# Layer 0 of a four-layer graph network: another opening, with the diagonal read from converted adjacency, the bias moved, wide loads of x and the table written by GpSimd

## Chip, cores and metric

The kernel runs on one core of one Trainium2 chip. The metric is the device time of one execution in microseconds (us). A core has five engines with queues of their own: TensorE (PE; its weight loads are listed as PEld), VectorE (DVE), ScalarE (ACT), GpSimd (POOL) and SyncE (SP). SP and ACT also issue transfers, which run on 16 DMA engines; GpSimd issues its own, and only it issues the indirect ones (gathers and scatters by a list of rows).

## What is computed

There are 3327 nodes with 256 values each (`x`) and a symmetric adjacency matrix of int32 with ones on its diagonal, about 1% full. Four attention layers follow each other, each as `x = layernorm(x + layer(x, adj))`. The change touches layer 0 alone:

```python
def _L0_gnn_ref(nodes, adj_mat, W_src_w, W_src_b, W_tgt_w, W_tgt_b, a_w):
    g_src = nodes @ W_src_w.T + W_src_b
    g_tgt = nodes @ W_tgt_w.T + W_tgt_b
    g = g_src[:, None, :] + g_tgt[None, :, :]
    g = jax.nn.leaky_relu(g, NEG_SLOPE)
    score = jnp.einsum('ijc,c->ij', g, a_w)
    score = jnp.where(adj_mat != 0, score, -jnp.inf)
    weights = jax.nn.softmax(score, axis=1)
    return weights @ g_tgt
...
x = _layernorm(x + _L0_gnn_ref(x, adj, ...), axis=-1)
```

The leaky relu stands inside the dot product with `a_w`, so a score can't be split into a part of i and a part of j. Layers 1 to 3 have scores that can, and are computed densely on the transposed adjacency.

## The kernel before

Layer 0 (`sparse0`, from L269) works on lists of neighbours. The rows are cut into 26 tiles of 128 (the last has 127), in four groups ("sets") of 4, 7, 9 and 6 tiles.

**The table.** `targets(it)` (L400) loads 128 columns of the transposed x on SP (`xt`, L386), projects them on TensorE (L391, product `pt`), adds the bias `bt_rows` on VectorE into `row` (L409), and ScalarE's queue writes the row to a table in DRAM (`table_d`, L410). For the first four tiles it is also written to `own0_d` (L412). `sources(it)` (L417) does the same with the other weight, adding its bias by a matmul with a row of ones (L396), and writes the negated product to the group's `own{s}_d` (L429). A row of `own{s}_d` holds the negated source, x and the target of one node. The x part is copied from DRAM to DRAM (L126 is the line of the helper `copy_rows`): on GpSimd's queue for the first group, on SP's for the others. The target part of the later groups is copied from the table by SP.

**The lists.** `neighbours(s)` (L462) is a generator. For each tile of its group it loads the adjacency rows in pieces of 1024 columns (SP, L126, `adj_i`, three buffers), ScalarE turns them into bf16 (L492, `adj_b`) and counts them, TensorE makes column numbers of the ones in banks of 512 columns (L502, L505; the node's own column is taken out by L510, product `v`, three PSUM buffers), and VectorE takes maxima of 8 over chunks of about 104 (`scan`, L522). `sort` (L525) draws the 56 largest from these, `note` (L537) makes the payload: the list, the node's number, and its diagonal flag from `own_marks`. The flag comes from `diag_i`, 3327 single elements of the adjacency loaded on ScalarE's queue (L351), which `mark_own` (L361) spreads. Then `key`, `spread_key` and `keep_key` make sort keys, and the nodes of a group are ranked by the number of their neighbours (L621), so that a tile needs only as many places as its fullest row. The first group's lists are put in order by matmuls (`permute`, L631), the others' by indirect writes and a read on GpSimd (`write_list`, `read_lists`).

**The gathers.** For each tile and each place k, GpSimd gathers 128 rows of the table (L730, 945 in all), four places to a part `g`, 22 buffers of a part. The own rows come by one gather for a tile (L718). VectorE forms `max(target, minus)` (L750) and its weighted sum (L756), ScalarE the exponentials and the scaled rows (L803), TensorE adds the rows up (L806). `add_input` (L826) adds the normalized sum to x; `put_back` (L840) scatters it to `sums{s}_d`. Gathers run 8 parts ahead of the scores. Small GpSimd work is put between two gathers through the list `between`, one item after every second gather (L736).

**What sets the order.** In layer 0 the order on TensorE, VectorE, ScalarE and GpSimd is the program's; SP's is left to a scheduler. The opening is the loop at L961: for each of the 26 tiles, `targets` is run to its end, and `next(first)` twice steps the first group's generator. Then the main loop at L1038 steps the generators of the later groups between the scores, as far as due times ask for it.

Of the kernel before, what the change touches and what calls it, by code (L numbers as in the profile page):

```python
# [8 lines left out]
F32 = mybir.dt.float32  # L9
# [40 lines left out]
def gat_stack(  # L50
# [218 lines left out]
    def sparse0(lost):  # L269
        GROUP, TURNS, LEAD, SPREAD = 4, 22, 8, 8  # L270
        starts = [sum(SETS[:s]) for s in range(len(SETS))]
        with ExitStack() as s0:
# [12 lines left out]

            w_tgt = const0.tile([P, kc, ROW], F32, name="w_tgt0")
            nc.sync.dma_start(w_tgt[:, :, :dim], w_tgt_t.rearrange("(c p) f -> p c f", p=P))
            nc.vector.memset(w_tgt[:, :, dim:], 0.0)
            a_row = load_row(const0, a_w, "a_row")
            bt_rows = const0.tile([P, ROW], F32, name="bt_rows")  # L290
            nc.vector.memset(bt_rows[:, dim:], 0.0)
            nc.sync.dma_start(
                bt_rows[:, :dim],
                bass.AP(tensor=b_tgt.tensor, offset=b_tgt.offset, ap=[[0, P], [1, dim]]),
            )
            w_src = const0.tile([P, kc, dim + 1], F32, name="w_src0")
            nc.scalar.dma_start(w_src[:, :, :dim], w_src_t.rearrange("(c p) f -> p c f", p=P))
            nc.vector.memset(w_src[:, :, dim:], 0.0)
            bs_row = const0.tile([1, dim + 1], F32, name="bs_row")
            nc.vector.memset(bs_row[:, dim:], BIG)  # L300
            nc.sync.dma_start(bs_row[:, :dim], b_src[None])
            for c in range(kc):
                t = io0.tile([P, dim], F32, tag="minus", name="dots0")
                nc.vector.tensor_mul(t, w_tgt[:, c, :dim], a_row)
                nc.vector.tensor_reduce(w_tgt[:, c, dim : dim + 1], t, axis=AX.X, op=ALU.add)
            nc.vector.tensor_scalar_mul(
                w_tgt[:, :, dim], w_tgt[:, :, dim], SLOPE
            )
            ones = const0.tile([P, P], F32, name="ones")
            nc.vector.memset(ones, 1.0)  # L310
            a_ps = ps0.tile([P, BANK], F32, tag="a", name="a_ps", bufs=1)
            nc.scalar.mul(a_ps[:, :dim], a_row, 1.0 - SLOPE)
            nc.scalar.copy(a_ps[:, dim : dim + 1], ones[:, :1])
# [5 lines left out]
            PIECE = 2 * BANK  # L319
            pieces = [(lo, min(n, lo + PIECE)) for lo in range(0, n, PIECE)]  # L320
            code = const0.tile([65, BANK], BF16, name="code")
            nc.vector.memset(code, 0.0)
            nc.vector.memset(code[64:65, :], 1.0)
            for row, pattern in ((0, [[16, BANK // 16], [0, 16]]), (32, [[0, BANK // 16], [1, 16]])):
                digit = io0.tile([P, PIECE], I32, tag="adj_i", name="digit", bufs=3)
                nc.gpsimd.iota(digit[:33, :BANK], pattern=pattern, base=0, channel_multiplier=0)
                nc.vector.tensor_copy(code[row : row + 1, :], digit[row : row + 1, :BANK])
# [5 lines left out]
            digit = io0.tile([P, PIECE], I32, tag="adj_i", name="digit", bufs=3)  # L333
# [13 lines left out]
            diag_i = const0.tile([P, nt], I32, name="diag_i")  # L347
            nc.vector.memset(diag_i, 0)
            for lo, hi in ((0, n // P), (n // P, nt)):
                if lo < hi:  # L350
                    nc.scalar.dma_start(  # L351
                        diag_i[: min(P, n - lo * P), lo:hi],
                        bass.AP(
                            tensor=adj.tensor, offset=adj.offset + lo * P * (n + 1),
                            ap=[[n + 1, min(P, n - lo * P)], [P * (n + 1), hi - lo]],
                        ),
                    )
# [3 lines left out]
            def mark_own():  # L361
# [100 lines left out]
            def neighbours(s):  # L462
# [121 lines left out]
                for k in all_pieces[:3]:  # L584
                    load(*k)
# [1264 lines left out]
```

## Time and profile before

| | us |
|---|---|
| median of three runs (3083.48 to 3091.56) | 3086.51 |
| the profiled execution | 3087.03 |
| its span, first to last instruction | 3085.2 |
| first conversion of adjacency on ScalarE (L492) starts | 30.76 |
| first gather of own rows (L718) starts | 128.25 |
| first gather of the table (L730) starts | 143.38 |
| last gather of the table starts | 1435.9 |
| last write-back of layer 0 (L843) starts | 1461.59 |

Lines of the timeline and of the chain of waits give a start and a length in us, then the engine (with a q behind it where its queue issues a transfer), the line of the kernel, the operation, output <- input, and how often; in brackets is the idle time before it and what ended it. A group of instructions has the mean length of one in ns behind its sum in us, then the idle time before such instructions with what ended it. A line of GpSimd's waits gives the sum in us, the number and the longest one. A line of windows gives, for each engine, busy us and number of instructions.

### The profile page before, as it was taken

How to read it: one execution, taken by the hardware profiler on the slowest of the kernel's cores; microseconds unless marked ns; L12 is line 12 of the kernel's file. 1: busy time of each engine (PE TensorE's matmuls, PEld its weight loads, DVE VectorE, ACT ScalarE, POOL GpSimd, SP SyncE). 2: the span in 40 equal slices, each digit the busy share in tenths (PEclk: the TensorE clock that was granted, in tenths of full speed). 3: DMA queues.
4: the chain of work that ended last, by engine and by line, in shares of the span. 5: the costliest groups of instructions: out<-in, count | busy, mean ns of one | idle time of the engine just before them, and what ended most of it. 6: DMA issues, size and time to landing. Idle time of an engine off the chain costs nothing.

```text
span 3085.2 us, 45364 instructions
## 1 busy us (share of the span) xinstructions
PE 2335.1 (76%) x16026; PEld 1293.6 (42%) x16046; DVE 2139.3 (69%) x5551; ACT 861.5 (28%) x2400; POOL 1014.8 (33%) x1073
## 2 busy tenths in 40 slices
PE   4547656544456423645899999989999999999996
PEld 2313222211222111322788888874434545434332
DVE  4499997777777536654355531129888889899997
ACT  1126544442344322534334421110110110120110
POOL 0177777777777777775000000000000000000000
PEclk8658768776677766868999999999999999999998
DMA  7676676455744436543776643341212212212211
GB/s 190 171 194 191 187 173 170 128 141 142 157 130 113 113 106 118 138 111 90 240 243 200 199 119 91 104 126 46 69 44 71 70 46 71 67 46 61 57 47 46
DMA packets 192883, 372.17 MB, mean 121 GB/s; under 512 B 38719, under 2 KB 135055, under 8 KB 191624
## 3 DMA queue, kind: packets, MB, share of 16 engines
q1 hardware_dynamic: 110668, 179.09, 20.8%
q0 software_dynamic: 51520, 156.84, 20.2%
q10 hardware_dynamic: 30460, 33.25, 3.2%
q8 instruction: 130, 2.13, 0.3%
q14 instruction: 105, 0.86, 0.1%
HBM read 329.27 MB, written 46.12 MB: 122 GB/s over the span
## 4 chain that ended last, share of the span: by engine, by line
PE 46%; DVE 4%; DMA 1%; issue 0%; ACT 0%; SPq 0%; POOL 0%; DVEq 0%; POOLq 0%; ACTq 0%
PE acc L1505 18%; PE acc L1458 16%; PE acc L1513 9%; PE misc L1304 3%; DVE e L1374 2%; DMA at<-at_d 1%; PE misc L1401 0%; PE misc L1587 0%; PE misc L1548 0%; DMA dst<-in_l_a_dram 0%; DVE stats L1665 0%; DVE h L1663 0%; DVE both L1660 0%; DVE h L248 0%; DVE h L1478 0%
## 5 line engine op out<-in xcount | busy, mean ns | idle before, releaser
L730 POOL DMA_INDIRECT g<-table_d,lst x945 | 898.0, 950 | 309.7 <-issue 256.3
L1374 DVE SCALAR_TENSOR_TENSOR e<-rate,feat,at 128x896 f32<-128x896 f32 (+4 forms) x832 | 844.1, 1079 | 80.8 <-PE acc L1513 69.7
L806 PE MATMUL acc<-g,ident 128*128 128x512 f32 x958 | 519.0, 688 | 353.8 <-ACT g L803 310.1
L1505 PE MATMUL acc<-e,feat 128*32 128x384 f32 (+2 forms) x6656 | 688.6, 516 | 4.8 <-DVE e L1374 2.1
L806 PEld LDWEIGHTS acc<-g,ident 128*128 128x128 f32 x958 | 203.2, 221 | 590.3 <-ACT g L803 462.4
L750 DVE TENSOR_TENSOR y<-g,minus_ps 128x1028 f32<-128x1028 f32 (+2 forms) x245 | 288.9, 1179 | 223.4 <-DMA g<-table_d,lst 211.9
L1505 PEld LDWEIGHTS acc<-e,feat 128*32 128x32 f32 x6656 | 259.3, 110 | 342.2 <-issue 231.4
L803 ACT ACTIVATE g<-g,w 128x256 f32<-128x256 f32 x945 | 389.5, 495 | 10.3 <-DMA h<-sums_d 4.9
L1513 PE MATMUL acc<-e,feat 128*32 128x384 f32 (+3 forms) x3328 | 375.4, 512 | 0.0
L756 DVE SCALAR_TENSOR_TENSOR y<-y,a_ps 128x257 f32<-128x257 f32 x945 | 342.7, 418 | 7.5
L1458 PE MATMUL acc<-feat,e 128*128 128x257 f32 (+2 forms) x1352 | 306.5, 384 | 16.2 <-DMA at_i<-in_adj_t_dram 13.3
L1458 PEld LDWEIGHTS acc<-feat,e 128*128 128x128 f32 (+2 forms) x1352 | 257.3, 192 | 54.4 <-issue 14.3
L242 POOL TENSOR_TENSOR rstds<-rstds,minus_half 128x7 f32<-128x7 f32 (+1 forms) x12 | 19.7, 1644 | 777.5 <-DVE rstds L241 777.5
L502 PE MATMUL v<-code,leads 65*128 65x512 bf16 (+1 forms) x182 | 84.5, 465 | 222.7 <-DVE cand L522 185.2
L1458 PE MATMUL acc<-feat,at 128*128 128x257 bf16 (+2 forms) x2028 | 239.6, 275 | 7.9 <-DMA at<-at_d 7.7
L1458 PEld LDWEIGHTS <-at 128*128 128x128 bf16 (+2 forms) x2028 | 199.6, 100 | 42.7 <-DMA at<-at_d 5.6
L1513 PEld LDWEIGHTS acc<-e,feat 128*32 128x32 f32 (+1 forms) x3328 | 139.6, 110 | 156.8 <-issue 132.7
L1374 DVE SCALAR_TENSOR_TENSOR e<-rate,feat,at_i 128x896 f32<-128x896 f32 (+2 forms) x104 | 111.6, 1080 | 75.2 <-DMA at_i<-in_adj_t_dram 43.0
L522 DVE MAX8 cand<-v 128x8 f32<-128x104 f32 (+2 forms) x858 | 158.6, 260 | 6.2 <-PE v L505 6.0
L1354 POOL DMA_DIRECT2D rate3b_d<-rate_rows x4 | 2.1, 524 | 468.3 <-ACT rate_rows L1353 468.3
L502 PEld LDWEIGHTS <-leads 65*128 65x128 bf16 x182 | 20.3, 112 | 260.3 <-DVE cand L522 210.9
L492 ACT ACTIVATE adj_b<-adj_i 128x1024 bf16<-128x1024 int32 (+1 forms) x104 | 92.5, 889 | 111.4 <-DMA diag_i<-in_adj_dram 23.5
(199 smaller groups left out, 1740.6 us busy)
## 6 DMA issues: line engine op xcount, KB each, us to landing
adj_i<-in_adj_dram SPq DMA_DIRECT2D x75, 512.0 KB, 4.6
at<-at_d SPq DMA_DIRECT2D x150, 224.0 KB, 2.5
at_i<-in_adj_t_dram SPq DMA_DIRECT2D x50, 448.0 KB, 4.6
g<-table_d,lst POOLq DMA_INDIRECT x945, 2.9
at<-at_d SPq DMA_DIRECT2D x75, 192.0 KB, 2.4
at<-at_d SPq DMA_DIRECT2D x75, 191.8 KB, 2.4
at_d<-at ACTq DMA_DIRECT2D x50, 224.0 KB, 4.2
at_i<-in_adj_t_dram SPq DMA_DIRECT2D x25, 384.0 KB, 3.4
```

The source lines that it names most:

```text
L502: nc.tensor.matmul(v[:, :w], leads[:, b, :], code[:, :w], start=True, stop=False)
L522: nc.vector.max(spread[:, c0 + c, :], view(v[:, :w]))
L730: nc.gpsimd.indirect_dma_start(out=g[:, k - k0, :], out_offset=None, in_=table_d[:, :], in_offset=bass.IndirectOffsetOnAxis(ap=entry["lst" ...
L750: nc.vector.tensor_tensor(y, rows, minus_src[:, None, :].to_broadcast([P, m, dim + 1]), op=ALU.max)
L756: nc.vector.scalar_tensor_tensor(y, y, 1.0, a_ps[:, : dim + 1], op0=ALU.mult, op1=ALU.mult, accum_out=sc)
L803: nc.scalar.activation(rows, rows, AF.Copy, scale=w[:, k : k + 1])
L806: nc.tensor.matmul(dst, ident, rows, start=start, stop=stop)
L1304: nc.tensor.matmul(pacc[:pn, : dim + self.extra], ht[:, k, :pn], self.weight[:, k, :], start=(k == 0), stop=(k == kc - 1),)
L1374: nc.vector.scalar_tensor_tensor(e[:pn, : c1 - c0], self.rate[b][:pn, h_of, : c1 - c0], q, at[:pn, : c1 - c0], op0=ALU.max, op1=ALU.mult,)
L1458: nc.tensor.matmul(accs[s][:pn, : dim + 1], a[:pj, s * P : s * P + pn], f[:pj, : dim + 1], start=(j == 0 and part == 0), stop=(j == nt - 1 ...
L1505: nc.tensor.matmul(accs[x][p][q : q + 32, : hi - lo], f[:pj, at0 : at0 + 32], es[at0 // hd][:pj, lo:hi], start=(j == 0), stop=(j == nt - 1),)
L1513: nc.tensor.matmul(accs[x][pairs][h_of * 32 : (h_of + 1) * 32, : hi - lo], f[:pj, dim + h_of : dim + h_of + 1].to_broadcast([pj, 32]), es[ ...
```

## The change

Six things are changed in layer 0, and nothing else:

- **Diagonal.** `diag_i`, its loads and `mark_own` are gone. In `fill`, VectorE multiplies the 128x128 block of converted adjacency on the diagonal with the identity and sums the rows into `own_marks`.
- **Bias of the targets.** It is no longer added to the table's rows. It is added to the sources' bias, and, since the weights of a row sum to one, to the x part of `own{s}_d`, by an accumulating transfer on GpSimd's queue: the first group's at the start, the others' between gathers.
- **Wide x.** In the opening x is loaded as seven pieces of 512 columns on ScalarE's queue, into buffers of the gathers that are needed last, instead of 128 columns at a time on SP's.
- **Table.** ScalarE copies the product to `row`; GpSimd's queue writes it.
- **Targets one behind.** The copy of tile `it` follows the matmuls of tile `it + 1`, and the generator is stepped once and twice in turn.
- **Adjacency first.** The first three pieces are the first transfers of SP's queue; weights, rows and biases move to ScalarE's. The iotas use another buffer.

```diff
+            for p in range(3):
+                load(0, 0, p)
             w_tgt = const0.tile([P, kc, ROW], F32, name="w_tgt0")
-            nc.sync.dma_start(w_tgt[:, :, :dim], w_tgt_t.rearrange("(c p) f -> p c f", p=P))
+            nc.scalar.dma_start(w_tgt[:, :, :dim], w_tgt_t.rearrange("(c p) f -> p c f", p=P))
...
+            def columns_wide(b):
+                lo, hi = banks_n[b]
+                t = gath.tile(
+                    [P, GROUP, ROW], F32, tag=f"g{(TURNS - 1 - b + SHIFT) % TURNS}", name="x_wide"
+                )
...
+                nc.scalar.dma_start(t[:, :, : hi - lo], x_t_p[:, :, lo:hi])
+            columns_wide(0)
             w_src = const0.tile([P, kc, dim + 1], F32, name="w_src0")
             nc.scalar.dma_start(w_src[:, :, :dim], w_src_t.rearrange("(c p) f -> p c f", p=P))
...
+            nc.scalar.dma_start(bias[:, 0, :dim], b_src[None])
+            nc.scalar.dma_start(bias[:, 1, :dim], b_tgt[None])
+            for b in range(1, len(banks_n)):
+                columns_wide(b)
...
-                    nc.scalar.dma_start(
-                        diag_i[: min(P, n - lo * P), lo:hi],
...
+            def keep_inputs(s, engine):
+                lo, hi = starts[s] * P, min(n, (starts[s] + SETS[s]) * P)
+                copy_rows(engine, own_d[s][: hi - lo, AT_X : AT_X + dim], x[lo:hi, :])
+
+            def add_bias(s):
+                lo, hi = starts[s] * P, min(n, (starts[s] + SETS[s]) * P)
+                nc.gpsimd.dma_start(
+                    own_d[s][: hi - lo, AT_X : AT_X + dim],
+                    b_tgt[None].to_broadcast([hi - lo, dim]), accum_op=ALU.add,
+                )
+
+            keep_inputs(0, nc.gpsimd)
+            add_bias(0)
...
+                nc.vector.tensor_add(bs_row[:, :dim], bs_row[:, :dim], bias[:, 1, :dim])
...
             def columns_of(it):
+                if not placed:
+                    b, at0 = divmod(it * P, BANK)
+                    return wide_x[b][:, :, at0 : at0 + pn], pn
...
-                nc.vector.tensor_add(row[:pn], pt[:pn, :ROW], bt_rows[:pn])
-                nc.scalar.dma_start(table_d[1 + it * P : 1 + it * P + pn, :], row[:pn])
+                nc.scalar.copy(row[:pn], pt[:pn, :ROW])
+                nc.gpsimd.dma_start(table_d[1 + it * P : 1 + it * P + pn, :], row[:pn])
...
+                        flag = io0.tile([P, P], BF16, tag="flag", name="flag", bufs=1)
+                        nc.vector.scalar_tensor_tensor(
+                            flag[:, :wo], adj_b[:, own0 % PIECE : own0 % PIECE + wo], 1.0,
+                            ident[:, :wo], op0=ALU.mult, op1=ALU.mult,
+                            accum_out=marks[:, starts[s] + t, 1:2],
+                        )
...
             first = neighbours(0)
+            next(first)
+            next(first)
+            score_columns()
+            waiting, turns = None, 0
             for it in range(nt):
-                if it == 3:
-                    mark_own()
-                for _ in targets(it):
+                row = targets(it)
+                next(row)
+                for _ in waiting or ():
                     pass
-                next(first, None)
-                next(first, None)
+                waiting = row
+                turns += 1 + it % 2
+                while turns:
+                    next(first, None)
+                    turns -= 1
+            for _ in waiting:
+                pass
...
             for s in range(1, len(SETS)):
-                copy_rows(nc.sync, own_d[s][: hi - lo, AT_X : AT_X + dim], x[lo:hi, :])
+                keep_inputs(s, nc.sync)
                 copy_rows(nc.sync, own_d[s][: hi - lo, AT_TGT:], table_d[1 + lo : 1 + hi, :])
+                at_step(4 + 2 * s, between.append, lambda s=s: add_bias(s))
```

`score_columns` holds what stood in line before: the dot products of the target weight with `a_w` and the two copies to `a_ps`.

## Prediction

> **What bounds the kernel now.** I read the page's slices first, then the chain of waits around the end of layer 0, then GpSimd's waits and the timeline of its first gathers, and last the work of the first 140 us.
>
> ```profile
> span 3085.2 us, 45364 instructions
> ...
> DVE  4499997777777536654355531129888889899997
> ...
> POOL 0177777777777777775000000000000000000000
> ```
>
> A slice is 77 us. GpSimd (POOL) works evenly from the second slice to the nineteenth: these are layer 0's row gathers. The chain of waits between 1400 and 1475 us starts at GpSimd's last write-back, and layer 1's loads and matmuls hang on it:
>
> ```profile
> 1461.59 2.41 DMA sums_d<-hs,lst
> ```
>
> ```profile
> 143.38 0.96 POOL L730 DMA_INDIRECT g<-table_d,lst  x1 [14.09 <-DMA table_d<-row]
> 144.65 0.95 POOL L730 DMA_INDIRECT g<-table_d,lst  x1 [0.30 <-issue]
> 145.90 0.95 POOL L730 DMA_INDIRECT g<-table_d,lst  x1 [0.30 <-issue]
> ```
>
> The timeline of GpSimd shows one gather every 1.256 us. 945 of them are 1187 us; with 26 own-row gathers, 26 write-backs and 22 list writes at about 1.3 us (96 us) that is 1283 us of the 1294 us from 143.4 to 1437.2. GpSimd's waits agree:
>
> ```profile
> POOL g L730 <- issue: 256.3, 842, 0.3
> ...
> POOL g L730 <- DMA g<-table_d,lst: 18.1, 35, 1.9
> POOL g L730 <- DMA table_d<-row: 14.1, 1, 14.1
> ```
>
> Only some 20 us of it is waiting for anything. So what starts the first gather earlier moves the end by as much, and what holds GpSimd up later costs its full length. Before the gathers no engine is full. The groups of instructions between 30 and 116 us and the timeline of ScalarE say why:
>
> ```profile
> L492 ACT ACTIVATE adj_b<-adj_i 128x1024 bf16<-128x1024 int32 (+1 forms) x16 | 14.3, 893 | 45.3 <-DMA diag_i<-in_adj_dram 23.5 <-DVE row L409 11.8 <-DVE cand L522 7.8
> ...
> L409 DVE TENSOR_TENSOR row<-pt,bt_rows 128x260 f32<-128x260 f32 x20 | 8.4, 423 | 51.8 <-PE pt L391 51.8
> ```
>
> ```profile
> 24.93 3.98 ACTq L351 DMA_DIRECT2D diag_i<-in_adj_dram  x1
> 29.00 0.58 ACTq L958 DMA_DIRECT2D table_d<-none  x1
> ```
>
> The first conversion of adjacency starts at 30.76 us, because ScalarE's queue is held by the loads of the diagonal; then VectorE stands 51.8 us before its 20 row additions, waiting for the targets' matmuls. Four tiles are scanned by 114.05 us, the list is ready and own rows are gathered at 128.25, and the first table gather waits until 143.38 for the table's last rows. The transfers of the opening are dense (last columns: granted clock, DMA share, GB/s):
>
> ```profile
> 5.00:10.00 5.00, 2.10 (x4) 1.17 (x4) 4.44 (x13) 0.46 (x2) 0.00 (x0) 1.00 1.04 260
> 10.00:15.00 5.00, 0.61 (x1) 0.13 (x2) 2.34 (x16) 0.00 (x0) 0.00 (x0) 1.00 1.15 214
> 15.00:20.00 5.00, 0.00 (x0) 0.00 (x0) 0.00 (x0) 0.00 (x0) 0.00 (x0) 1.00 1.10 205
> 20.00:25.00 5.00, 0.00 (x0) 0.00 (x0) 0.00 (x0) 0.00 (x0) 0.00 (x0) 1.00 1.19 214
> 25.00:30.00 5.00, 0.00 (x0) 0.00 (x0) 0.00 (x0) 0.00 (x0) 0.00 (x0) 1.00 1.00 275
> ```
>
> **What the Trainium skill says.** "DMA: Bandwidth & Descriptors", on why a DMA increments its semaphore by 16: a transfer of 127 partitions from SP or ScalarE runs on one DMA engine, while GpSimd spreads some such copies over 16. The trace agrees with the first half: the table's last write, 127 rows, is issued at 134.33 and releases GpSimd 9.05 us later; the median of the other table writes is 2.5. The second half no run shows yet. The same page, on issuing engines, says that all queues end on the same 16 DMA engines; the shares above 1.0 fit. "Collectives: The Full Stack", on the bandwidth ceiling: an add inside a DMA reads two sources, so such transfers ran at half the rate (ratio 1.93). No accumulating transfer is in this trace. "TensorE: Matmul & The Clock Gate", part 1: an idle TensorE falls to half clock. The trace shows it: the 512-column scan matmul takes 0.38 us at best and 0.63 at other times.
>
> **The change, part by part.** All sums are made on the profiled execution, 3087.03 us (span 3085.2), which stands 0.5 us above the median of 3086.51.
>
> *The start of scanning.* The diagonal's two loads, of 4-byte pieces, go. The adjacency stands first on SP's queue, but ScalarE now issues 13 transfers ahead of its first conversion: weights, rows and seven wide loads of x. SP and ScalarE share eight completion counters, and a transfer is issued only when the one that last had its counter has landed. The instruction order of the built kernel pairs the fourth wide load with own1's copy of x, the fifth with the last piece of own3's, the seventh with SP's first narrow load. So ScalarE cannot convert until own3's copy has landed. Until then there must land: adjacency 1.57 MB, own1 to own3 2.88, weights and a_row 0.66, four wide loads 2.10, own0 0.52 and its bias 0.52 counted one and a half times (below), 8.5 MB. At 250 GB/s, between the windows' 205 and 275 and nearer their top because the 4-byte pieces are gone, that is 34 us, with 2 us before the first bytes 36; then four issues (2 us) and the activation table (1.28): first conversion at 39.5, 9 us later than now. Ends: 35 (300 GB/s) and 46 (210).
>
> *Scanning.* Removed from VectorE: 26 row additions at 0.43 (11 us) and the wait for the matmuls ahead of each. ScalarE takes the copies, 26 at about 0.4, beside 1.1 us conversions; in the hundred us it has about 30 us of work, so this is hidden. "One behind" puts the next target's matmuls before the copy, so neither engine waits for its own product. VectorE keeps per tile 33 maxima at 0.18 (6.0), the sort (5.1), the note (0.5) and gains one diagonal product of 128x128 (about 0.35): 12.0 us. The four tiles took 15.5 (35.62 to 51.1), 23.9, 18.9 and 20.1. TensorE's work per tile is about 10 us at the fast clock and 20 at the slow, and it still idles in each sort. I take 14.5 per tile, from 12 (VectorE alone) to 18: 58 us, with 5 us from first conversion to first maximum as now.
>
> *List and table.* From the last note to the own-row gather the trace has 14.2 us (114.05 to 128.25), of which about 1 us is a row addition and its wait: 13. The table's 31 writes go to GpSimd, which is idle here, at about 1.3 us each; with three row buffers a target needs no more than 4 us from copy to landing, and the last is copied before the list is done. The one-engine write goes. So the first gather follows the own rows by 1.4 us: 39.5 + 5 + 58 + 13 + 1.4 = 117, where it was 143.4: **26 us gained**; with the ends of both terms 6 to 41.
>
> *Bias into sources and inputs.* One small addition on VectorE and row bs_row: nothing. But the inputs of the groups get the bias by accumulating transfers from GpSimd. own0's is in the opening. Those of 896, 1152 and 767 rows are pushed between gathers, about 8 gathers apart, from the 54th on. Each takes GpSimd about 1.1 us plus 0.3 (the 512-row copy took 0.84, the list reads 1.03): **4.2 us lost**. Then they lie in the same software queue as the gathers. GpSimd's transfers use eight counters too, so the eighth issue after an accumulation, 1.4 + 7 x 1.256 = 10.2 us on, waits for it to land. Landing: 0.92, 1.18 and 0.79 MB, taken 1.5 times as between a copy (1) and the page's two reads (2), at 60% of 210 GB/s because adjacency loads use the engines too, plus 2 us: 12.9, 16.0 and 11.4. Stalls 2.7 + 5.8 + 1.2 = **9.7 us lost**. At factor 1: about 1 (8 to 12 us each, under the slack). At 2: 6 + 11 + 4 = 21. At 3: 14 + 20 + 10 = 44. These rates are the least certain numbers here.
>
> *The rest.* 22 diagonal products in VectorE's gather stage, 0.35 each, 8 us in 1290, in which VectorE is 72% busy; between 160 and 300 it is at 95%, and 2 us there eat into the lead of 8 parts, not into GpSimd. The count of the diagonal moves behind the last sum: 0.2 us. SP loses 30 narrow loads; its adjacency loads no longer stand behind ones that wait for TensorE, but its table copies still wait for GpSimd's writes: no cost while a tile's loads stay ahead.
>
> Sum: -26.4 + 4.2 + 9.7 + 0.2 = -12.3 us: **3074**.
>
> **Rivals.** (1) The stalls eat the gain: factor 2 with a first gather at 120: -23 + 4 + 21 = +2, 3089, no change to be measured (0.3%, 9.3 us, is what a measurement of this kernel tells apart). For it: the page's ratio; the gathers take 5.7 us to land, not 2.9, between 195 and 245, just where the accumulations fall. Against: much of that window's traffic comes in bursts. (2) Slower: one mechanism, the accumulations on GpSimd's queue. At three times a copy they land after 24, 30 and 20 us: -23 + 4 + 44 = +25, 3112. It decides from a factor of 2.3 on, where the sum is +9. Every row is a read, an add and a write of 1 KB, and if these don't overlap on an engine that price is near. (3) No stalls, conversions at 37 and 13 us per tile, first gather at 109: -34 + 4 + 1 = -29, 3058; for it: the first tile in the trace took 15.5 with the fast clock. (4) The opening doesn't become shorter: conversions at 46 and 18 us per tile give a first gather at 137: -6 + 4 + 10 = +8, 3095. For it the transfers that stand ahead of ScalarE's work; against, the 51.8 us of waits that are taken out.
>
> **How the numbers follow.** Forecast 0.38, (1) 0.24, (2) 0.18, (3) 0.12, (4) 0.08. The forecast's own range is 3064 to 3084, so about a quarter of it falls within 0.3%. Faster: 0.29 + 0.12 + 0.05 from low ends of (1) = 0.46. Same: 0.09 + 0.17 + 0.05 = 0.31. Slower: 0.18 + 0.03 + 0.02 = 0.23. Range: from (3) to just short of (2), 3057 to 3106.
>
> **What will show it.** First conversion (ScalarE, adj_b) near 39 us, later than now. VectorE without waits for pt; tiles some 14 us apart. First g gather near 117, 1.4 us after own rows. Around the 54th to 78th gather, three accumulating transfers and behind each a wait of GpSimd for a transfer of 1 to 6 us; the interval of gathers elsewhere 1.256. The last write-back near 1449, and all behind it shifted alike. Wrong if the first gather is past 130, or if the three waits together pass 25 us.

## Result, and the profile after

The changed kernel takes 3106.57 us (median, 3105.89 to 3106.82), the kernel before beside it 3084.99: the ratio is 1.0066 with a 95% interval of 1.0049 to 1.0084. It is slower by about 20 us, where 12 us of gain were forecast.

The page's slices of the profiled execution show the same shape as before, with an engine at work earlier and for longer:

```profile
span 3104.8 us, 45392 instructions
...
POOL 1455777777777777776000000000000000000000
```

GpSimd (POOL) now has work from the first slice, the table's writes, and its gathers reach one tenth further into the slice where they end. The start of the gathers, on its timeline:

```profile
115.04 0.56 POOL L452 DMA_DIRECT2D table_d<-row  x1 [0.35 <-ACT row L451]
115.59 0.52 POOL L456 DMA_DIRECT2D own_d<-row  x1
125.28 1.06 POOL L744 DMA_INDIRECT own_of<-own_d,lst  x1 [9.18 <-DVE flag L547]
126.65 0.97 POOL L756 DMA_INDIRECT g<-table_d,lst  x1 [0.30 <-issue]
```

The first table gather comes at 126.65 us, 16.7 earlier than before. It follows the own rows by 1.37 us without any wait: the last write of 127 rows, on GpSimd's queue, was done in time. So the opening gave a gain, smaller than the 26 us of the forecast. How large, one trace tells to some 5 us: in the versions below with the same opening the first table gather comes between 121.83 and 126.97 us. The chain of waits shows that it is gone by the end of layer 0; the last write-back, which was at 1461.59, has moved later by 25.5:

```profile
1487.07 2.37 DMA sums_d<-hs,lst
```

Between the first and the last gather lie 1334.1 us, where it was 1292.6. GpSimd's waits name the 42 us (sum, number, longest one):

```profile
POOL g L756 <- DMA own_d<-in_b_tgt_dram: 42.1, 3, 17.2
...
POOL g L756 <- DMA g<-table_d,lst: 11.9, 32, 1.6
```

and its timeline shows each of the three accumulations with the stall behind it:

```profile
201.03 1.38 POOL L392 DMA_DIRECT2D own_d<-in_b_tgt_dram  x1 [0.59 <-DMA g<-table_d,lst]
...
230.19 0.95 POOL L756 DMA_INDIRECT g<-table_d,lst  x1 [15.96 <-DMA own_d<-in_b_tgt_dram]
...
231.90 1.50 POOL L392 DMA_DIRECT2D own_d<-in_b_tgt_dram  x1 [0.76 <-issue]
...
259.51 0.94 POOL L756 DMA_INDIRECT g<-table_d,lst  x1 [17.21 <-DMA own_d<-in_b_tgt_dram]
260.44 1.36 POOL L392 DMA_DIRECT2D own_d<-in_b_tgt_dram  x1
279.61 0.94 POOL L756 DMA_INDIRECT g<-table_d,lst  x1 [8.92 <-DMA own_d<-in_b_tgt_dram]
```

Behind each accumulation GpSimd issues seven more gathers, then it stands until the accumulation has landed. The landings are in the list of transfers (size, then us from issue to landing):

```profile
own_d<-in_b_tgt_dram POOLq DMA_DIRECT2D x1, 1152.0 KB, 27.4
own_d<-in_b_tgt_dram POOLq DMA_DIRECT2D x1, 896.0 KB, 28.9
own_d<-in_b_tgt_dram POOLq DMA_DIRECT2D x1, 767.0 KB, 18.9
...
own_d<-in_b_tgt_dram POOLq DMA_DIRECT2D x1, 512.0 KB, 23.2
```

The balance: 16.7 earlier at the start, against 42.1 of stalls and 4.2 for the three issues, less 6.2 because gathers wait less for gathers (11.9 us where it was 18.1). That gives 23.4 us; the last gather is in fact 24.8 later (1460.75 against 1435.94). The span grew by 19.6 only, since what follows the last gather took 1644.0 us where it was 1649.3. That part of the kernel is the same in all versions below, and in those on this chip it scatters between 1641 and 1649 without order, so the difference can't be put down to the change.

The opening itself, on the timeline of ScalarE:

```profile
5.56 37.88 ACTq L330 DMA_DIRECT2D x_wide<-in_x_t_dram  x6
43.53 0.28 ACTq L984 DMA_DIRECT2D table_d<-none  x1
43.84 1.28 ACT L524 ACT_TABLE_LOAD   x1 [43.84 <-DMA xt<-in_x_t_dram]
45.14 1.06 ACT L524 ACTIVATE adj_b<-adj_i 128x1024 bf16<-128x1024 int32 x1
```

The issue of six wide loads takes ScalarE's queue 38 us, and the first conversion of adjacency starts at 45.14, 14 us later than before. From there the four tiles take until 111.75. The 51.8 us that VectorE waited for the targets' product are gone; what it waits for in the tiles is the scan's product, 12.9 us:

```profile
DVE flag L547 <- ACT adj_b L524: 44.0, 4, 38.6
DVE cand L560 <- PE v L537: 12.9, 10, 1.9
```

In part the waits have moved to ScalarE, which copies the product now: between 30 and 116 us it stands 16.2 us for `pt` and 10.2 for writes of the table that still hold a `row`.

### The profile page after: what moved, and what is told of

Read it like the earlier page. It is cut to its first block, busy times and chain, and to the rows that moved or that the text cites. A ratio compares the mean times of both kernels' runs of the same rounds, so it can differ in the third digit from the quotient of the medians.

```text
span 3104.8 us, 45392 instructions
## 1 busy us (share of the span) xinstructions
PE 2339.8 (75%) x16046; PEld 1294.9 (42%) x16046; DVE 2137.5 (69%) x5575; ACT 869.1 (28%) x2426; POOL 1036.3 (33%) x1108
## 3 DMA queue, kind: packets, MB, share of 16 engines
q0 software_dynamic: 56384, 164.24, 22.0%
## 4 chain that ended last, share of the span: by engine, by line
PE 46%; DVE 4%; DMA 1%; issue 1%; ACT 0%; SPq 0%; POOL 0%; POOLq 0%; DVEq 0%; ACTq 0%
PE acc L1545 18%; PE acc L1498 16%; PE acc L1553 9%; PE misc L1344 3%; DVE e L1414 2%; DMA at<-at_d 1%; DMA at_i<-in_adj_t_dram 1%; PE misc L1441 0%; PE misc L1627 0%; PE misc L1588 0%; DVE stats L1705 0%; DVE h L1703 0%; DVE both L1700 0%; DVE h L248 0%; DVE h L1518 0%
## 5 line engine op out<-in xcount | busy, mean ns | idle before, releaser
L832 PE MATMUL acc<-g,ident 128*128 128x512 f32 x958 | 526.5, 696 | 350.5 <-ACT g L829 321.7
L1498 PE MATMUL acc<-feat,e 128*128 128x257 f32 (+2 forms) x1352 | 305.0, 383 | 15.2 <-DMA l3aw<-in_l_w_dram 14.1
L1431 ACT CAST at<-at_i 128x896 bf16<-128x896 int32 (+2 forms) x104 | 92.0, 885 | 104.3 <-DMA at_i<-in_adj_t_dram 88.3
```

Of the source, the lines that this page charges most:

```text
L832: nc.tensor.matmul(dst, ident, rows, start=start, stop=stop)
L1498: nc.tensor.matmul(accs[s][:pn, : dim + 1], a[:pj, s * P : s * P + pn], f[:pj, : dim + 1], start=(j == 0 and part == 0), stop=(j == nt - 1 ...
```

## The experiments

All versions stand side by side here. "Landings" are those of the transfers in the place of the three late accumulations (896, 1152 and 767 rows, a dash where the trace has none), "stalls" GpSimd's waits for them in sum. Before was measured again beside each group of versions: 3084.99 beside after, 3088.94 beside e1 to e4, 3087.96 beside e5 and e8 to e10, 3086.74 beside e6, e7, e11 and e12. So medians of different groups may be set side by side within 4 us, and the ratios are free of this. e13 and e14 ran on another chip, on which the kernel before took 3496.03 and the gathers stood longer for other engines; of those two only the ratio and the opening are used.

| | median us | ratio to before (interval) | first conversion | first gather | landings | stalls |
|---|---|---|---|---|---|---|
| before | 3084.99 | | 30.76 | 143.38 | | |
| after | 3106.57 | 1.0066 (1.0049–1.0084) | 45.14 | 126.65 | 28.9, 27.4, 18.9 | 42.1 |
| e1 no late adds | 3065.51 | 0.9929 (0.9912–0.9945) | 44.02 | 125.95 | | |
| e4 before + late adds | 3130.74 | 1.0135 (1.0118–1.0152) | 31.21 | 142.35 | 28.6, 26.7, 18.4 | 40.6 |
| e2 plain, one row | 3105.46 | 1.0056 (1.0040–1.0073) | 44.28 | 121.83 | –, 23.3, 16.4 | 34.8 |
| e8 add, own rows | 3072.41 | 0.9956 (0.9942–0.9970) | 43.23 | 122.49 | 20.0, 12.9, 9.2 | 9.6 |
| e9 plain, own rows | 3075.82 | 0.9956 (0.9939–0.9973) | 44.87 | 126.97 | –, –, 8.2 | 4.9 |
| e10 add from SBUF | 3074.45 | 0.9958 (0.9942–0.9975) | 44.80 | 126.33 | –, –, 7.6 (640 rows) | 10.2 |
| e5 adds by tiles | 3086.39 | 0.9998 (0.9990–1.0007) | 43.63 | 123.06 | 5.9 (median) | 3.4 |
| e3 bias on VectorE | 3056.58 | 0.9894 (0.9877–0.9910) | 34.43 | 115.90 | | |
| e11 first add, own rows | 3056.43 | 0.9902 (0.9886–0.9917) | 36.59 | 116.44 | | |
| e12 all adds from SBUF | 3068.30 | 0.9938 (0.9923–0.9953) | 36.71 | 117.51 | –, –, 7.6 (640 rows) | 9.1 |
| e6 wide loads by GpSimd | 3057.37 | 0.9904 (0.9889–0.9919) | 33.91 | 114.84 | | |
| e7 and copies later | 3039.67 | 0.9844 (0.9830–0.9857) | 13.22 | 96.76 | | |
| e13 copies by GpSimd | | 0.9935 (0.9917–0.9953) | 13.19 | 109.77 | | |
| e14 copies later alone | | 0.9908 (0.9883–0.9933) | 21.42 | 102.99 | | |

### What the three accumulations cost: e1 and e4

```diff
 e1 (from after)
-                at_step(4 + 2 * s, between.append, lambda s=s: add_bias(s))
 e4 (from before)
...
+                at_step(4 + 2 * s, between.append, lambda s=s: add_bias(s))
```

e1:

> The changed kernel without the three accumulating transfers between the gathers; the first group's stays. Left out: the bias in the x part of the later groups. Theory A (these three transfers hold the gathers' queue): GpSimd's three waits of 42 us and 4 us of issuing go, the first table gather stays at 126 to 127 us, and the time falls by about 46 us from 3106.6, to 3058 to 3070. Rival B (the gathers of that stretch are held up by adjacency loads and VectorE anyway, the accumulations only show where): the waits move to other transfers, and the time stays within 15 us of 3106, 3092 to 3107.

e4:

> The kernel before with the same three accumulating transfers at the same places among the gathers, and nothing else. Changed in the computation: the later groups' x part gets the bias a second time. Theory A: each holds the gathers as in the changed kernel, 35 to 50 us in all with 4 us of issuing: 3120 to 3138. Rival C (they only cost because the changed opening makes them collide with the adjacency loads and table copies): under 15 us, 3085 to 3100.

Taking them out of the changed kernel gives back 41.1 us; putting them into the kernel before costs 41.8 against the 3088.94 measured beside it, with landings and stalls like those of after. The loss is theirs, and it does not depend on the rest of the change.

### Is it the add? e2

```diff
...
+            def write_beside(s):
...
+                nc.gpsimd.dma_start(
+                    beside[s][: hi - lo, AT_X : AT_X + dim],
+                    b_tgt[None].to_broadcast([hi - lo, dim]),
+                )
...
-                at_step(4 + 2 * s, between.append, lambda s=s: add_bias(s))
+                at_step(4 + 2 * s, between.append, lambda s=s: write_beside(s))
```

> The changed kernel with the three transfers at the same places, from the same one row of bias, with the same shape and row pitch, but as plain writes into a DRAM tensor that nobody reads. Left out: the bias in the x part of the later groups. Theory A1 (the add inside the transfer is what takes 19 to 29 us): they land in 8 to 13 us, GpSimd waits less than 8 us in all for them, 3062 to 3076. Rival A2 (a DRAM to DRAM transfer of 767 to 1152 rows from one source row takes that long on GpSimd's queue, add or not): landing stays above 18 us, waits above 30 us, 3097 to 3108.

The same rows, written without adding into a scratch tensor, cost nearly the same: 3105.46. They land somewhat sooner than with the add (23.3 and 16.4 us where it was 27.4 and 18.9, the second below the 18 of rival A2). GpSimd's waits, in the trace of e2:

```profile
POOL g L767 <- DMA beside_d<-in_b_tgt_dram: 34.8, 3, 13.9
```

So the add, with its second read, is not what makes them long, and the prediction's reason for a slow transfer falls. What is left in common is the source, one row of the bias that every row of the transfer reads, and the queue.

### Is it the source? e8, e9 and e10

e8 adds and e9 writes the rows of x, each from its own place in HBM (the chip's DRAM); e10 adds the bias from SBUF (the core's memory on the chip), where it stands once in each of 128 partitions.

```diff
 e8
...
+                nc.gpsimd.dma_start(
+                    own_d[s][: hi - lo, AT_X : AT_X + dim], x[lo:hi, :], accum_op=ALU.add
+                )
...
 e9
...
+                nc.gpsimd.dma_start(beside[s][: hi - lo, AT_X : AT_X + dim], x[lo:hi, :])
...
 e10
...
+                nc.gpsimd.dma_start(
+                    own_d[s][: full * P, AT_X : AT_X + dim].rearrange("(t p) d -> p t d", p=P),
+                    bt_rows[:, None, :].to_broadcast([P, full, dim]), accum_op=ALU.add,
+                )
...
```

e8:

> As the changed kernel, but the three late accumulations take as source the rows of x of their own group, each row read from its own place in HBM, in place of the one row of the bias that all rows read. Rows, bytes, targets, queue and places in the program stay. It leaves out the bias of the targets for groups 1 to 3 and adds x a second time there. Theory S (the one source row is what makes them slow: every row of the transfer reads the same kilobyte): landings near 8 to 13 us, GpSimd waits for them under 10 us in sum, median 3063 to 3078. Theory Q (a transfer from HBM to HBM on GpSimd's queue is that slow among the gathers, whatever it reads): landings 18 to 29 us, waits 30 to 45 us, median 3098 to 3112.

e9:

> As the changed kernel, but in place of the three late accumulations the rows of x of the group are written, without adding, into a scratch tensor with the rows' pitch of own_d. It leaves out the targets' bias for groups 1 to 3. With e2 (plain, one source row), the changed kernel (add, one source row) and e8 (add, own source rows) it fills a square of add against source. Theory S: landings 8 to 12 us, waits under 8 us, median 3062 to 3075. Theory Q: landings 16 to 24 us as in e2, waits 25 to 40 us, median 3095 to 3108.

e10:

> As the changed kernel, but the three late accumulations read the bias from SBUF, where it stands once in each of 128 partitions (bt_rows, loaded at the start by GpSimd's queue), and no longer from HBM; they still add in HBM, on GpSimd's queue, at the same places; the last group's 767 rows go as two transfers. All of the reference is computed. Theory S: landings 8 to 13 us, waits under 10 us, median 3065 to 3080. Theory Q in its wide form (any adding or plain transfer of a thousand rows on that queue is slow): landings 18 to 29 us, median 3098 to 3112.

From 3106.57 all three fall to between 3072 and 3076, e9 a little above its range, e10 with stalls of 10.2 us where under 10 were expected. The square is filled: with one source row 3106.57 (add) and 3105.46 (plain), with own rows 3072.41 (add) and 3075.82 (plain). In these medians the add can't be seen, since the opening and what follows layer 0 scatter by more. The stretch from the first to the last gather is free of both: in the traces it takes 1334.1 (add) and 1330.6 us (plain) with one source row, 1302.0 and 1299.8 with own rows. The source is worth 31 to 32 us there, the add 2 to 4. So the source decides, and the add is a small part. That the rows of x lie one behind another doesn't let GpSimd's queue move them in fewer packets: after and e8 have 56384 packets and 164.24 MB on it, e2 and e9 54272 and 164.24.

The timeline of GpSimd in e8, against that of after above, has the same three issues 21.8 and 14.1 us apart, where it was 30.9 and 28.5:

```profile
197.00 1.38 POOL L399 DMA_DIRECT2D own_d<-in_x_dram  x1 [0.93 <-DMA g<-table_d,lst]
...
217.22 0.95 POOL L762 DMA_INDIRECT g<-table_d,lst  x1 [6.91 <-DMA own_d<-in_x_dram]
218.75 1.51 POOL L399 DMA_DIRECT2D own_d<-in_x_dram  x1 [0.59 <-issue]
231.89 0.94 POOL L762 DMA_INDIRECT g<-table_d,lst  x1 [2.73 <-DMA own_d<-in_x_dram]
232.82 1.36 POOL L399 DMA_DIRECT2D own_d<-in_x_dram  x1
```

The first landing, 20.0 us, is above the 8 to 13 expected; around 200 us the other transfers are dense as well (before, the gathers took 5.7 us to land there). The windows of 204 to 229 us (last three columns: granted clock, DMA share, GB/s) tell what one source row does to the DMA engines. In after:

```profile
204.00:229.00 25.00, 14.54 (x31) 6.16 (x30) 17.83 (x87) 11.73 (x32) 6.80 (x7) 0.50 0.95 167
```

and in e8:

```profile
204.00:229.00 25.00, 17.71 (x38) 7.68 (x39) 23.89 (x114) 14.54 (x39) 13.38 (x14) 0.61 1.08 257
```

The engines are nearly as full in one as in the other, but they move 167 GB/s in after and 257 in e8. GpSimd's queue alone had 1319 packets and a share of 65.4% in this window of after, 2575 and 72.7% in e8; from these I estimate 0.20 us of an engine's time for a packet in after and 0.11 in e8, with some 1560 and 1390 bytes in each. So a packet that reads the one row seems to hold an engine longer than its bytes explain. What makes such reads slow, no run here shows.

### Is it the wait or the engines' time? e5

```diff
...
-                at_step(4 + 2 * s, between.append, lambda s=s: add_bias(s))
+                for t in range(SETS[s]):
+                    at_step(4 + s, between.append, lambda s=s, t=t: add_bias(s, t, t + 1))
```

> As the changed kernel, source row included, but the three late accumulations are cut into 22 of up to 128 rows, one between two gathers from the same place on; all of the reference is computed. Theory D (the loss is the wait for one long transfer, because the eighth issue after it waits for its landing; the engines' time alone would be hidden): each piece lands in 2.5 to 5 us, within the slack of some 10 us, waits for own_d under 6 us in sum, and what is paid is 22 issues of about 1.25 us less three of 1.35: the version without the late accumulations (3065.5) plus some 27, 3085 to 3098. Theory E (the DMA engines' time is paid, since the gathers stand behind the rows on the same rings): the gathers wait as long as before in smaller parts, and the issues come on top: 3110 to 3135.

3086.39, inside theory D's range; the pieces take 5.9 us to land, above the 2.5 to 5 expected. The same rows from the same single source row no longer stop GpSimd, because nearly every small piece lands within the slack before a later issue needs it. (The edit also lets the pieces begin a little sooner, 69 us after the first gather where the first accumulation of after stands 74 us behind it.) In the trace of e5, GpSimd's group and its waits:

```profile
L392 POOL DMA_DIRECT2D own_d<-in_b_tgt_dram x23 | 23.2, 1009 | 11.4 <-DMA own_d<-in_x_dram 7.9 <-DMA g<-table_d,lst 3.2 <-issue 0.2
```

```profile
POOL g L756 <- DMA own_d<-in_b_tgt_dram: 3.4, 3, 1.7
```

What is paid is the issues: 22 pieces of 1.0 us and 0.3 between are 29, against the 20.9 us between e1 and e5. The traces close the sum: from the first to the last gather e5 takes 1314.8 us and e1 1291.8, 23.0 less, and that is 29 for the issues and 3.4 for the waits, less 9.1 because gathers wait less for gathers (12.6 us where e1 has 21.7). The first gather was 2.9 earlier here.

### The opening: e3, e11 and e12

e3 has no accumulations; VectorE adds the bias to each tile's result. e11 is e1 with the first accumulation from the rows of x. e12 is e10 with the first accumulation from SBUF.

```diff
 e3
-            add_bias(0)
+            bt_rows = const0.tile([P, dim], F32, name="bt_rows")
+            nc.gpsimd.dma_start(
+                bt_rows, bass.AP(tensor=b_tgt.tensor, offset=b_tgt.offset, ap=[[0, P], [1, dim]])
+            )
...
+                nc.vector.tensor_add(y, y, bt_rows)
...
-                at_step(4 + 2 * s, between.append, lambda s=s: add_bias(s))
 e11 (from e1)
-            add_bias(0)
+            nc.gpsimd.dma_start(
+                own_d[0][: SETS[0] * P, AT_X : AT_X + dim], x[: SETS[0] * P, :],
+                accum_op=ALU.add,
+            )
 e12 (from e10)
-            add_bias(0)
+            add_rows(0)
```

e3:

> The changed kernel without any accumulating transfer: one row of bias is spread over 128 partitions at the start, and VectorE adds it after the residual, 26 additions of 128x256. Theory A: 26 x 0.4 us lie beside the gathers, about 0.5 us of it at the very end; the time is that of the run without late bias, within 4 us, 3058 to 3072, and below the kernel before (3085). Rival: VectorE is full between 130 and 340 us (95% in the kernel before), and the additions push it over: 3072 to 3085.

e11:

> As e1 (no late accumulations), but the first accumulation too, that of group 0 at the start, reads the rows of x, each from its own place, and no longer the one bias row. It leaves out the targets' bias altogether and adds x twice in group 0. Theory S carried to the opening (512 reads of one row keep the DMA engines full while the wide loads of x wait on the same engines, so that ScalarE's queue, and with it the first conversion at 44 to 45 us, is late): landing of that accumulation near 9 us, first conversion 35 to 38 us, first table gather 116 to 120 us, median 3056 to 3061 (e1 3065.5, e3 without the transfer 3056.6). Theory N (the opening is late because of the wide loads and copies themselves): first conversion and first gather as in e1, 3063 to 3068.

e12:

> As e10, with the first accumulation from the SBUF copy of the bias too, so that no transfer of many rows reads the one row in HBM, apart from the load of bt_rows itself, 128 reads. All of the reference is computed. Theory S: first conversion 35 to 39 us, first gather 116 to 121 us, and some 8 less than e10's 3074.5: median 3063 to 3070. Theory N: as e10, 3071 to 3078.

e3 is faster than both kernels by more than the intervals, and falls below the range that I had given it. Against e1 it gains 8.9 us that no late accumulation explains; e11 gains the same with one edit, the source of the first accumulation, and its first conversion and first gather move with it. On e1's timeline of ScalarE, from 20 us on (four of the six wide loads are issued after that):

```profile
23.23 19.08 ACTq L330 DMA_DIRECT2D x_wide<-in_x_t_dram  x4
...
44.02 1.06 ACT L524 ACTIVATE adj_b<-adj_i 128x1024 bf16<-128x1024 int32 x1
```

and on e11's:

```profile
20.90 13.93 ACTq L330 DMA_DIRECT2D x_wide<-in_x_t_dram  x4
...
36.59 1.06 ACT L527 ACTIVATE adj_b<-adj_i 128x1024 bf16<-128x1024 int32 x1
```

The windows of 24 to 34 us show where the time goes. In e1, after and e11, in this order:

```profile
24.00:34.00 10.00, 0.00 (x0) 0.00 (x0) 0.00 (x0) 0.00 (x0) 0.00 (x0) 1.00 0.80 134
```

```profile
24.00:34.00 10.00, 0.00 (x0) 0.00 (x0) 0.00 (x0) 0.00 (x0) 0.00 (x0) 1.00 1.02 112
```

```profile
24.00:34.00 10.00, 0.00 (x0) 0.00 (x0) 0.00 (x0) 0.00 (x0) 0.00 (x0) 1.00 1.10 246
```

With 512 reads of one row among their work, until 35.8 and 37.4 us, the engines move 134 and 112 GB/s here; in e11, where the same transfer has landed by about 23, they move 246. So theory S holds in the opening as to the source. Its other half, that the reads keep the engines full, is not shown: the share is 1.02 in after, but 0.80 in e1. By first gathers alone the gain is less sure than by conversions: the seven versions with the bias row in the opening have 121.83 to 126.97 us, e3, e11 and e12 115.90 to 117.51. e12 is the change with only the source of its accumulations mended: 3068.30, all of the reference computed, and still 12 us behind e3 for the stalls of 9.1 us and the issues.

### What else holds the first conversion: e6, e7, e13 and e14

```diff
 e6 (from e3)
-                nc.scalar.dma_start(t[:, :, : hi - lo], x_t_p[:, :, lo:hi])
+                engine = nc.gpsimd if b else nc.scalar
+                engine.dma_start(t[:, :, : hi - lo], x_t_p[:, :, lo:hi])
 e7 (from e6), e14 (from e3)
-                keep_inputs(s, nc.sync)
+                at_step(2 * s, keep_inputs, s, nc.scalar)
 e13 (from e6)
             keep_inputs(0, nc.gpsimd)
+            for s in range(1, len(SETS)):
+                keep_inputs(s, nc.gpsimd)
...
-                keep_inputs(s, nc.sync)
```

e6:

> As e3 (bias added by VectorE, no accumulations), but the wide loads of x after the first two are issued by GpSimd's queue in place of ScalarE's. All of the reference is computed. Theory T (the six issues on ScalarE's queue hold the first conversion at 34.4 us, and the engines could start sooner): first conversion 24 to 29 us, first gather 106 to 111 us, median 3046 to 3052. Theory U (the DMA engines are full in the first 40 us, and what the first tiles need comes no sooner): first gather 113 to 118 us, median 3054 to 3060.

e7:

> As e6, and the copies of the x rows of groups 1 to 3 (2.8 MB from HBM to HBM) leave SP's queue in the opening and are issued by ScalarE among the gathers of group 0. All of the reference is computed. Theory U: with that traffic gone the first gather comes 5 to 10 us before that of e6, and the gathers of group 0 lose little for it: median 3046 to 3053. Theory V (the opening is held by something other than transfers, or the copies cost among the gathers what they cost before them): within 3 of e6.

e13:

> As e6, and the copies of the x rows of groups 1 to 3 stay in the opening, but GpSimd's queue issues them behind its own of group 0, in place of SP's: the same bytes at about the same time, without a completion counter in common with ScalarE's transfers. All of the reference is computed. Theory C (ScalarE's queue waits for a counter that one of these copies holds): first conversion 12 to 18 us as in e7; the tiles after it are slower than e7's for the traffic, first gather 98 to 110 us, median 3040 to 3052. Theory B (their bytes delay what the conversion needs): first conversion 27 to 35 us as in e6, first gather 112 to 118 us, median 3053 to 3060.

e14:

> As e3, with the x rows' copies of groups 1 to 3 issued by ScalarE among the gathers of group 0, and the wide loads left on ScalarE's queue in the opening. All of the reference is computed. Theory C and B alike: most of what e7 gained is kept, since e6 alone gained nothing; with six wide issues on the queue, which wait for counters of xt and of each other, first conversion 17 to 26 us, first gather 98 to 106 us, median 3039 to 3047. If the wide loads on ScalarE's queue hold it as they did before: first conversion above 30 us, median 3053 to 3058.

e6 has the times of theory U, and theory T falls: with the six loads gone (all but the first, not all but two as the expectation says) from ScalarE's queue the first conversion stayed at 33.91. ScalarE's timeline in e6 shows that its queue is empty from 5.5 us on and that the next thing on it, the one-row write of the table, goes out at 32.36 only; what came last was a copy of x rows:

```profile
5.30 0.24 ACTq L339 DMA_DIRECT2D bias<-in_b_tgt_dram  x1
32.36 0.23 ACTq L989 DMA_DIRECT2D table_d<-none  x1
32.62 1.28 ACT L528 ACT_TABLE_LOAD   x1 [32.62 <-DMA own_d<-in_x_dram]
33.91 1.06 ACT L528 ACTIVATE adj_b<-adj_i 128x1024 bf16<-128x1024 int32 x1
```

In e7, without those copies in the opening:

```profile
11.66 0.23 ACTq L989 DMA_DIRECT2D table_d<-none  x1
11.92 1.28 ACT L528 ACT_TABLE_LOAD   x1 [11.92 <-DVE none L988]
13.22 1.06 ACT L528 ACTIVATE adj_b<-adj_i 128x1024 bf16<-128x1024 int32 x1
```

That came sooner than I had expected (13.22, and the first gather 18 us before e6's, where 5 to 10 were expected), so e7 had taken away two things, the copies' bytes and a completion counter that one of them held. e13 leaves the bytes and moves the copies to another queue, which issues them between 9 and 16.3 us, where SP's issued them from 4.8 to 24.7:

```profile
11.63 0.23 ACTq L991 DMA_DIRECT2D table_d<-none  x1
11.90 1.28 ACT L530 ACT_TABLE_LOAD   x1 [11.90 <-DVE none L990]
13.19 1.06 ACT L530 ACTIVATE adj_b<-adj_i 128x1024 bf16<-128x1024 int32 x1
```

With the same bytes the first conversion is at 13.19: what held it in e6 was the copy that ScalarE's next transfer had to wait for, not the traffic: theory C, and U's times in e6 did not come from U's reason. But the traffic seems to be paid by the next tile. The first gather of e13 is at 109.77, only 5 us before e6's (on another chip, where the opening of e6 or e7 was not traced), and ScalarE's waits have one of 18.4 us for adjacency:

```profile
ACT adj_b L530 <- DMA adj_i<-in_adj_dram: 19.0, 2, 18.4
```

In e7 this wait is 5.0 at most. So the copies cost twice, once by their counter and, as far as these traces tell, once by their bytes, and moving them among the gathers takes off both. They cost little there: from the first to the last gather e7 takes 1300.1 us and e6 1294.4, some 6 us for a first gather 18 us sooner. e14 keeps the wide loads on ScalarE's queue: first conversion at 21.42 and first gather at 102.99, inside the ranges expected, which puts the wide loads' own share at some 6 to 8 us once the copies are gone. Whether e14's time is near e7's, its chip doesn't let one say.

## Why the prediction was wrong, point by point

*What bounds the kernel: right.* GpSimd's queue carries layer 0, and what holds it up costs its full length: 42.1 us of stalls in after, 41 us gained in e1.

*The landing of the accumulations: the step that failed.* For the time of a landing the prediction took "1.5 times as between a copy (1) and the page's two reads (2)", landings of 12.9, 16.0 and 11.4 us, stalls of 9.7. Measured: 28.9, 27.4 and 18.9, stalls of 42.1. The slack of 10.2 us was right: in after seven gathers go out behind each accumulation and the next one waits, and in e8 the landing of 9.2 us causes no wait. What was left out is that all rows read one kilobyte; e8 shows what that was worth, with landings of 20.0, 12.9 and 9.2 and stalls of 9.6. That these stalls and e8's median of 3072.41 come so near the forecast of 9.7 and 3074 is in part chance: the stalls were foretold as 2.7, 5.8 and 1.2 and came as 6.9, 2.7 and none. The prediction counted bytes and engines; the profile of before held a row that could have warned, in its list of transfers:

```profile
w_tgt<-in_w_tgt_t_dram SPq DMA_DIRECT2D x1, 256.0 KB, 3.5
...
a_row<-in_a_w_dram SPq DMA_DIRECT2D x1, 128.0 KB, 3.6
```

`a_row` is one row read 128 times, and it took as long as twice the bytes beside it. The Trainium skill, "Collectives: The Full Stack", on the bandwidth ceiling, from which the factor came, speaks of a reduce that reads two sources. Here an accumulation took 1.12 to 1.18 times as long to land as the plain write in its place (9.2 and 8.2 us with own rows, 27.4 and 23.3, 18.9 and 16.4 with one row), neither 1.5 nor 2.

*The first conversion: mechanism right, size wrong.* 39.5 was taken, 45.14 came, just inside the 35 to 46 (whose lower end is 34 by its own sum). That ScalarE's queue waits for own3's copy agrees with the trace of after: the copy's large piece goes out at 12.88 us and takes 28.9 to land, until 41.8, and the fifth wide load goes out at 42.02. e6 and e13 show a wait of this kind by experiment. The size was off by the same omission: the first accumulation was put in as half a megabyte "counted one and a half times", 3 us at 250 GB/s, and its source row costs 7.4 us of first conversion (e1 against e11); own3's piece took 28.8 us to land in e1 and 21.5 in e11.

*The tiles.* 14.5 us each was taken; first maximum to last note came to 63.1 us, 15.8 each, inside 12 to 18. VectorE's waits for `pt` are gone as forecast, and it waits for the scan's product instead, 12.9 us. That "neither engine waits for its own product" was wrong for ScalarE, which stands 16.2 us for `pt` and 10.2 for a free `row`; that this delays the scan is likely, but no run shows it. With 3.5 us from conversion to first maximum (5 taken) and 13.5 to the own rows (13 taken), the first gather is at 126.65 in place of 117: 9.7 us, 5.6 by the conversion and 5.1 by the tiles, with 1 back. e11 returns 9.5 against e1, of which only 7.4 is conversion; the rest lies within the scatter of first gathers.

*The table on GpSimd: right.* The last write of 127 rows no longer delays a gather; 1.4 us between own rows and table, as forecast. The Trainium skill, "DMA: Bandwidth & Descriptors", on why a DMA increments its semaphore by 16, has GpSimd spread some such copies over all 16 engines. The trace agrees as far as it goes: this one landed 2.4 us after its issue, where ScalarE's took 9.05; on how many engines it ran, I have not read from a trace.

```profile
table_d<-row POOLq DMA_DIRECT2D x1, 129.0 KB, 2.4
```

*The issues: right.* 1.38, 1.50 and 1.36 us busy, 4.2 in sum.

*The sum.* -12.3 became about +20 by two terms: 32.4 for the stalls and 9.7 for the opening, with about 10 back from gathers that wait less for each other (6.2) and from the scatter of what follows layer 0. The rival that was slower came near in number, with stalls of 44 and 3112, but that was luck: its reason, the add's read, add and write on an engine, fell with e2. Of the two signs that were to show the prediction wrong, the first gather stayed short of 130 us and the three waits went past 25.

## What to carry to other kernels

A broadcast from HBM, where hundreds of rows of a transfer read the same short row, should not be priced by its bytes; among the gathers here it took 1.4 to 2.1 times as long to land as rows of their own. Replicate the row in SBUF first, or put the addition on an engine with time to spare, as e3 does with VectorE. A long transfer on a queue that also feeds the critical path stops that path when its completion is asked for some issues later; cut into pieces that land within the slack it cost its issues here and 3.4 us of waits. And a copy that nobody needs soon should not stand in the opening, where it can hold both the engines' time and a completion counter of someone else's queue: e7, the fastest of the versions on this chip, is e3 with the wide loads on another queue and these copies later, 3039.67 us, a ratio of 0.9844 (0.9830 to 0.9857).

## What the runs showed of the hardware that I had not expected

Accumulations of 512 to 1152 rows of 1 KB, all read from one row of HBM, took 18 to 29 us to land; from rows of their own in the same places 9 to 20. While one of the first kind was under way, the share of the DMA engines was 0.80 to 1.02 and all transfers together moved 112 to 167 GB/s; in the same windows with rows of their own it was 1.08 and 1.10, with 257 and 246 GB/s. Adding in the transfer made the landing 1.12 to 1.18 times as long as a plain write's. From SBUF as the source, 640 rows were added in 7.6 us.
